# Ten gather buffers instead of six in a four-layer convolution kernel, with shorter projection blocks and two blocks' denominators in one tile

## Chip, cores and metric

The kernel is one program on one core of a Trainium2 chip. The metric is device time in microseconds (us) of one execution, the median of the runs. Engines are called by the profile's names: PE (matrix multiply), DVE (vector), ACT (scalar), POOL (here it only issues gathers), SP (issues all other transfers).

## What is computed

The input is `x`, 4 images of 256 channels on a 64x64 grid, all float32. Four layers follow each other, each of the form `x = x + layer(groupnorm(x))`:

```
layer 0: y  = leaky(bn(conv1x1(x)))
         xp = inproj(y)                       # the table that is sampled
         t  = leaky(bn(depthwise3x3(y)))
         offset, mask = off(t), softmax(mask(t))       # 4 groups x 9 points per pixel
         d  = sum over points of mask * bilinear(xp, base + offset)   # the gather
         x2 = bn(y + outproj(d)); x3 = x2 * se(mean(x2)); y + fc2(leaky(fc1(x3)))
layer 1: q, k, v = relu(bn(conv1x1(x))), and a depthwise 5x5 of each
         out = (v k^T) q / (sum(k) q + eps)   # linear attention, heads of 8 channels
         relu(bn(proj(out)))
layer 2: conv3x3 with binarised weights
layer 3: attention with keys and values max-pooled 2x2, then conv1x1
```

## The kernel before

One image at a time goes through the layers, and work of different images is interleaved. `prepare` makes, for an image, the convolution, the table that is sampled (`tab`, in DRAM: every row holds two vertically adjacent pixels of one group, 512 bytes, and a gather reads two neighbouring rows) and for every sampling point an index and four weights (`s_d`). `sample` gathers and weights. `feedforward` is the rest of layer 0, then come `layer1`, `layer2` and `layer3`.

`run` sets which work lies beside which: `sample(0)` beside `prepare` of images 1 to 3; `sample(1)` beside `first(0)` (feed-forward and layer 1 of image 0); `sample(2)` beside `first(1)` and `second(0)` (layers 2 and 3); `sample(3)` beside `first(2)` and `second(1)`; then `first(3)` beside `second(2)`, and last `second(3)`. `beside` runs the generators in turn: after each step of `sample` (a *unit*), the other works are advanced until their own costs catch up. From this traced order, the dependences and its own estimates a scheduler fixes one instruction order for each engine, and it is not changed at run time. Waits on semaphores are added where they are needed.

`sample` in detail. The pixels of an image are cut into blocks of `BP = RP * BR` pixels (L28 to L30); a *round* is `RP = 14` pixels with 9 points each, so 126 points on the partitions; a unit is `UR = 4` rounds. The 4096 pixels make 293 rounds and 74 units an image. For a block SP loads indices and weights (`sl`, L445, L446) and the residual (`yb`, L448). For a round, POOL issues four indirect transfers (one a group, L465) into one buffer `g` of 4 KB a partition; PE multiplies it with the weights `wm` (made by DVE for a unit, L458), 8 small products a round, 32 a unit, into the PSUM tile `acc` (L472). ACT copies `acc` to `at` (L475), PE transposes it into `dp` (L478), ACT copies that into `dT` (L486). At the end of a block PE multiplies `dT` with the output projection into `po` (L493, two times four products; `po` shares its one PSUM buffer with `dp`), DVE adds it to `yb` (L495), ACT applies the batch norm (L496) and SP stores the block (L498). The tiles `yb` and `dT` have one buffer each, `sl` and `wm` two, `g` six.

`layer1` in detail. A 5x5 depthwise filter (`aggregate`, L600 to L606) is a chain of 25 DVE instructions (L171, L169) into one PSUM tile `agg`, then an ACT copy (L605) into a tile `ak` or `av`, two buffers each. There are 24 of these an image. For the attention output, each chunk of 16 image rows has two blocks `h` of 512 pixels. A block makes a denominator of 64 rows (four products into `den`, L664), adds eps (L666) and takes the reciprocal (L667) on DVE, then for each of four channel groups a product `num` (L671), a product that spreads the reciprocals with the 0/1 matrix `sel` (`rden`, L673), an ACT copy (L674) and a DVE multiplication (L675); the projection follows (L679).

Of the kernel before, what the change touches and what calls it, by code (L numbers as in the profile page):

```python
# [7 lines left out]
F32 = mybir.dt.float32  # L8
I32 = mybir.dt.int32
AF = mybir.ActivationFunctionType  # L10
ALU = mybir.AluOpType
# [4 lines left out]
P = 128  # L16
N, C, H, W = 4, 256, 64, 64
HW = H * W
KT = C // P
NB = HW // 512  # L20
NT = HW // P
G, PT = 4, 9
# [2 lines left out]
NCH = NT // CT  # L25


RP, UR, BR = 14, 4, 36  # L28
RS, BP = RP * PT, RP * BR
BLOCKS = [(p0, min(BP, HW - p0)) for p0 in range(0, HW, BP)]  # L30
OB = 16
# [9 lines left out]
EPS_ATT = 1e-5  # L41
# [24 lines left out]
class Net:  # L66
# [366 lines left out]
    def sample(self, n, ssum):  # L433


        nc, sp = self.nc, self.sp2
        table = self.tab[n].rearrange("g y x s c -> (g y x) (s c)")
        for b, (p0, np_) in enumerate(BLOCKS):
            sl = sp.tile([P, BR, G * 5], F32, name="sl")
            whole, part = np_ // RP, np_ % RP  # L440

            nr = whole + (part > 0)
            rows = self.s_d[n][p0 * PT:p0 * PT + nr * RS, :].rearrange("(r p) f -> p r f", p=RS)
            more = self.s_d[n][p0 * PT + RS:p0 * PT + (nr + 1) * RS, :].rearrange("(r p) f -> p r f", p=RS)
            nc.sync.dma_start(sl[0:RS, 0:nr], rows)  # L445
            nc.sync.dma_start(sl[RS:P, 0:nr], more[0:P - RS])  # L446
            yb = sp.tile([P, KT, BP], F32, name="yb", bufs=1)
            nc.sync.dma_start(yb[:, :, 0:np_], self.y_d[n][:, :, p0:p0 + np_])  # L448
            dT = sp.tile([P, G, BP], F32, name="dT", bufs=1)
            rounds = [(r, RP) for r in range(whole)] + [(whole, part)] * (part > 0)  # L450
            for u in range(0, len(rounds), UR):
                unit = rounds[u:u + UR]
                nu = len(unit)

                wm = self.gp.tile([P, UR, 4 * G, OB], F32, name="wm")
                sh = [P, nu, 4 * G, OB]

                self.tc.keep_in_program_order(nc.vector.tensor_tensor(  # L458
                    wm[:, 0:nu], self.con("own").unsqueeze(1).unsqueeze(1).to_broadcast(sh),
                    sl[:, u:u + nu, G:].unsqueeze(3).to_broadcast(sh), ALU.mult))  # L460
                acc = self.ps1.tile([P, UR, P], F32, name="acc")
                for v, (r, m) in enumerate(unit):
                    g = self.gp.tile([P, G, 256], F32, name="g", bufs=6)
                    for i in range(G):
                        nc.gpsimd.indirect_dma_start(  # L465
                            out=g[:, i, :], out_offset=None, in_=table,
                            in_offset=bass.IndirectOffsetOnAxis(ap=sl.bitcast(I32)[:, r, i:i + 1], axis=0))


                    for x in range(2):  # L470
                        for i in range(G):
                            nc.tensor.matmul(acc[32 * i:32 * i + 32, v, :], wm[:, v, 4 * i + 2 * x:4 * i + 2 * x + 2, :],  # L472
                                             g[:, i, x * P:(x + 1) * P], start=x == 0, stop=x == 1)
                at = sp.tile([P, UR, P], F32, name="at", bufs=1)
                nc.scalar.copy(at[:, 0:nu], acc[:, 0:nu])  # L475
                dp = self.ps1.tile([P, UR, G, 2, OB], F32, name="dp", tag="dp")
                for v in range(nu):
                    nc.tensor.transpose(dp[:, v].rearrange("p g s o -> p (g s o)"), at[:, v], self.ident)  # L478

                full = sum(1 for _, m in unit if m == RP)  # L480
                for v0, v1, m in ((0, full, RP), (full, nu, unit[-1][1])):
                    for s in range(2):
                        if v0 < v1:
                            hs = slice(64 * s, 64 * s + 64)
                            q0 = RP * (u + v0)
                            nc.scalar.copy(  # L486
                                dT[hs, :, q0:q0 + m * (v1 - v0)].rearrange("p g (v o) -> p g v o", o=m),
                                dp[hs, v0:v1, :, s, 0:m].rearrange("p v g o -> p g v o"))
                yield 1
            for m in range(KT):  # L490
                po = self.ps1.tile([P, 512], F32, name="po", tag="dp")
                for k in range(G):
                    nc.tensor.matmul(po[:, 0:np_], self.ow[:, k, m * P:(m + 1) * P], dT[:, k, 0:np_], start=k == 0, stop=k == G - 1)  # L493
                ym = yb[:, m, 0:np_]
                nc.vector.tensor_tensor(ym, po[:, 0:np_], ym, ALU.add)  # L495
                nc.scalar.activation(ym, ym, AF.Identity, bias=self.sh[:, 4 + m:5 + m],  # L496
                                     scale=self.inv[:, 4 + m:5 + m], accum_out=ssum[:, m, b:b + 1])
            nc.sync.dma_start(self.x2_d[n][:, :, p0:p0 + np_], yb[:, :, 0:np_])  # L498
# [51 lines left out]
    def layer1(self, n, st, st2):  # L550
# [3 lines left out]
        with tc.tile_pool(name=f"la{n}", bufs=1, side="right") as sp, \  # L554
# [45 lines left out]
            def aggregate(pd, i, name, func, **more):  # L600

                acc = self.ps1.tile([P, 16, W], F32, name="agg", tag="agg")
                self.depthwise(acc, pd, self.w5[:, i], 5, 16, W, 0, bias=self.b5[:, i:i + 1])
                v = bp.tile([P, 16, W], F32, name=name, tag=name)
                nc.scalar.activation(v, acc, func, **more)  # L605
                return v  # L606

# [41 lines left out]
            for got in rows((0, 1), None, 8):  # L649
                if not isinstance(got, tuple):  # L650
                    yield got
                    continue
                c, qp = got
                aq = []
                for t in range(2):
                    aq.append(aggregate(qp[t], t, ("ak", "av")[t], AF.Relu))
                    yield 28
                for h in range(2):
                    b = 2 * c + h
                    xv = self.block(bp, self.x3_d[n], b, "xr")  # L660
                    qs = [q[:, 2 + 8 * h:10 + 8 * h, 2:W + 2] for q in qp] + [v[:, 8 * h:8 * h + 8, :] for v in aq]
                    pd = self.ps("den")
                    for j in range(4):
                        nc.tensor.matmul(pd[0:64], ld[:, j], qs[j], start=j == 0, stop=j == 3)  # L664
                    rd = bp.tile([64, 512], F32, name="rd", tag="v1")
                    nc.vector.tensor_scalar(rd, pd[0:64], EPS_ATT, None, ALU.add)  # L666
                    nc.vector.reciprocal(rd, rd)  # L667
                    ot = [bp.tile([P, 512], F32, name="ot", tag="kt", bufs=4) for _ in range(4)]
                    for j in range(4):
                        pn = self.ps("num")  # L670
                        nc.tensor.matmul(pn, ln[:, j], qs[j], start=True, stop=True)  # L671
                        pb = self.ps("rden")
                        nc.tensor.matmul(pb, self.con("sel")[0:64, j * P:(j + 1) * P], rd, start=True, stop=True)  # L673
                        nc.scalar.copy(ot[j], pn)  # L674
                        nc.vector.tensor_tensor(ot[j], ot[j], pb, ALU.mult)  # L675
                    for m in range(KT):
                        ps = self.ps()
                        for j in range(4):
                            nc.tensor.matmul(ps, pw[:, j, m * P:(m + 1) * P], ot[j], start=j == 0, stop=j == 3)  # L679
                        r = bp.tile([P, 512], F32, name="pr", tag="v0")  # L680
                        nc.scalar.activation(r, ps, AF.Relu, bias=self.vec("proj_b", m), scale=self.vec("proj_s", m))
                        nc.vector.tensor_tensor(xv[:, m], xv[:, m], r, ALU.add)
                    self.stats(st2, xv, b)
                    nc.sync.dma_start(self.x4_d[n][:, :, b * 512:(b + 1) * 512], xv)
                    yield 20
# [35 lines left out]
    def layer3(self, n, st):  # L721
        nc, tc, a = self.nc, self.tc, self.a
        M = HW // 4
        with tc.tile_pool(name=f"na{n}", bufs=1, side="left") as sp, \
# [32 lines left out]
            for b in range(NB):  # L757
# [3 lines left out]
                    nc.tensor.matmul(ps, tw[:, k], x[:, k], start=k == 0, stop=k == KT - 1)  # L761
                nc.scalar.activation(th[:, b * 512:(b + 1) * 512], ps, AF.Identity, bias=tb)

                m1 = bp.tile([P, KT, 256], F32, name="m1", bufs=1)
                v = x.rearrange("p k (x d) -> p k x d", d=2)
                nc.vector.tensor_tensor(m1, v[:, :, :, 0], v[:, :, :, 1], ALU.max)
                v = m1.rearrange("p k (r d x) -> p k r d x", d=2, x=W // 2)
                xq = bp.tile([P, KT, P], F32, name="xq")
                nc.vector.tensor_tensor(xq.rearrange("p k (r x) -> p k r x", x=W // 2),
                                        v[:, :, :, 0], v[:, :, :, 1], ALU.max)  # L770
                ps = self.ps()
# [101 lines left out]
def arrays(x, **w):  # L873
# [27 lines left out]
    for k in ("theta_b", "phi_b", "wz_b"):  # L901
# [13 lines left out]
        "by": (p[:, None, None] // W + 2 * np.arange(CT)[None, :, None] + d[point % 3][None, None]).reshape(P, -1),  # L915
        "gi": np.broadcast_to((q // PT) * TY * TX + TX + 1, (P, Q)),
        "own": p[:, None] // PT == np.arange(OB)[None],
        "sel": (p[:, None, None] == 16 * np.arange(4)[None, :, None] + p[None, None] // 8).reshape(P, -1),
    }
    rows = np.concatenate([w[l0 + "inproj_b"], w[l0 + "off_b"], w[l0 + "mask_b"], w[l3 + "g_b"]])  # L920
    return {
# [36 lines left out]
```

## Time and profile before

| | us |
|---|---|
| median of 3 runs | 12207.65 (12192.76 to 12220.47) |
| the profiled execution, its own time | 9745.96 |
| its span, first to last instruction | 9744.2 |
| busy in it: PE, DVE, POOL, ACT | 6706.8, 5358.5, 4553.3, 1820.3 |
| mean granted clock of PE, share of full speed | 0.778 |
| gathers in it | 4688, first start 258.0, last start 7349.7 |
| bytes moved | 1052.37 MB, 58% of them by gathers |

The profiled execution is 20% shorter than the median of the runs. A stage below is one image's gathers: S0 from 258 to 1802 us, S1 to 3379, S2 to 5344, S3 to 7351; then the tail to 9744. "Busy" is the union of the instructions' times on an engine. A wait "A <- B" is idle time of A's engine that the end of B ended; its columns are the total in us, the number of times, and the longest in us.

### The profile page before, as it was taken

What the parts mean: (1) busy time and instruction counts of PE and PEld (TensorE: products, weight loads), DVE (VectorE), ACT (ScalarE), POOL (GpSimd) and SP (SyncE); (2) the same over time, 40 slices, a digit from 0 to 9 for tenths busy, and PEclk for the clock granted to TensorE, in tenths of its full rate; (3) what the DMA queues carried; (4) which work ended last, traced back from release to release, by engine and by line L of the source; (5) the groups of instructions that cost most, each with busy time, mean ns of one, the idle gap of its engine ahead of it and who ended that gap; (6) DMA issues with size and microseconds to landing.
All of it is one profiled execution on the core that took longest, in us unless ns stands there. A gap on an engine that the chain in (4) does not pass through costs nothing. (4 is left out here: it accounts for less than half of the span.)

```text
span 9744.2 us, 89537 instructions
## 1 busy us (share of the span) xinstructions
PE 6706.8 (69%) x34636; PEld 3559.7 (37%) x34636; DVE 5358.5 (55%) x6359; ACT 1820.3 (19%) x3546; POOL 4553.3 (47%) x4694
## 2 busy tenths in 40 slices
PE   3567676775557599756676997655778955356797
PEld 2333333343323244333343443333343423233345
DVE  7643444347776624667656226677563287775413
ACT  1111111122211122122221211122121112111112
POOL 0677777777677745656656355656551000000000
PEclk7766677786767799877777897877778977677799
DMA  5665655544335444434333443434332111001110
GB/s 153 174 181 155 169 153 159 149 144 124 114 112 145 119 126 132 113 105 117 108 111 112 127 131 109 118 112 117 100 113 83 61 32 41 15 28 33 42 56 31
DMA packets 795242, 1052.37 MB, mean 108 GB/s; under 512 B 462144, under 2 KB 502208, under 8 KB 793024
## 3 DMA queue, kind: packets, MB, share of 16 engines
q0 software_dynamic: 225024, 614.77, 21.9%
q1 hardware_dynamic: 569792, 431.88, 15.3%
q8 instruction: 273, 4.47, 0.2%
q14 instruction: 153, 1.25, 0.0%
HBM read 878.36 MB, written 167.90 MB: 107 GB/s over the span
## 5 line engine op out<-in xcount | busy, mean ns | idle before, releaser
L465 POOL DMA_INDIRECT g<-tab,sl x4688 | 4552.6, 971 | 2796.7 <-issue 1324.2
L169 DVE SCALAR_TENSOR_TENSOR agg<-pad,vec,agg 128x1024 f32<-128x1024 f32 x2560 | 3294.2, 1287 | 65.5 <-ACT pad L356 1.2
L472 PE MATMUL acc<-g,wm 128*32 128x128 f32 x18752 | 1351.0, 324 | 856.1 <-DMA g<-tab,sl 715.6
L472 PEld LDWEIGHTS acc<-g,wm 128*32 128x32 f32 x18752 | 744.2, 124 | 1569.1 <-DMA g<-tab,sl 1139.2
L711 PE MATMUL ps<-xp,w 128*128 128x512 f32 x2304 | 1025.0, 598 | 20.8 <-ACT xp L705 20.8
L711 PEld LDWEIGHTS ps<-xp,w 128*128 128x128 f32 x2304 | 432.2, 191 | 534.4 <-issue 513.0
L617 PE MATMUL pt<-ident,av 128*128 128x128 f32 x256 | 88.9, 405 | 767.1 <-ACT av L605 767.1
L475 ACT COPY at<-acc 128x512 f32<-128x512 f32 (+1 forms) x296 | 172.1, 581 | 2224.4 <-PE acc L472 2224.0
L536 PE MATMUL ps<-x2f,f 128*128 128x512 f32 x1024 | 466.9, 607 | 5.1 <-ACT f L528 5.1
L458 DVE TENSOR_TENSOR wm<-con,sl 128x1024 f32<-128x1024 f32 (+1 forms) x296 | 354.4, 1207 | 199.8 <-PE acc L472 199.7
L543 PE MATMUL ps<-hm,f 128*128 128x512 f32 x1024 | 453.4, 594 | 0.0
L160 DVE SCALAR_TENSOR_TENSOR hm<-ps,vec,lk 128x512 f32<-128x512 f32 x256 | 192.2, 751 | 441.6 <-ACT lk L159 438.4
L801 PE MATMUL pt<-ident,pe 128*128 128x128 f32 x1024 | 201.8, 342 | 331.1 <-ACT pe L794 330.2
L806 PE MATMUL ps<-gt,pT 128*128 128x128 f32 x2048 | 392.5, 368 | 32.7 <-DVE pT L803 26.4
L582 PE MATMUL ps<-xr,qw 128*128 128x512 f32 x768 | 390.7, 638 | 6.4 <-DMA xr<-x 6.4
L159 ACT ACTIVATE lk<-ps,low 128x512 f32<-128x512 f32 x320 | 219.7, 687 | 929.4 <-PE ps L536 615.2
L806 PEld LDWEIGHTS ps<-gt,pT 128*128 128x128 f32 x2048 | 363.4, 274 | 76.0 <-DVE pT L803 68.8
L171 DVE TENSOR_SCALAR agg<-pad,vec,b 128x1024 f32<-128x1024 f32 x96 | 129.0, 1344 | 414.6 <-ACT pad L352 272.3
L617 PEld LDWEIGHTS pt<-ident,av 128*128 128x128 f32 x256 | 53.7, 214 | 778.6 <-ACT av L605 778.6
L715 DVE TENSOR_TENSOR x<-x,ps 128x512 f32<-128x512 f32 x64 | 43.9, 686 | 480.9 <-PE ps L711 480.9
L478 PE MATMUL dp<-ident,at 128*128 128x128 f32 x1172 | 234.9, 334 | 100.2 <-ACT at L475 99.6
L801 PEld LDWEIGHTS pt<-ident,pe 128*128 128x128 f32 x1024 | 142.0, 171 | 435.3 <-ACT pe L794 432.6
(225 smaller groups left out, 7418.5 us busy)
## 6 DMA issues: line engine op xcount, KB each, us to landing
x<-x SPq DMA_DIRECT2D x160, 512.0 KB
g<-tab,sl POOLq DMA_INDIRECT x4688
xr<-x SPq DMA_DIRECT2D x128, 512.0 KB
x<-in_x SPq DMA_DIRECT2D x64, 512.0 KB
tab<-xo SPq DMA_DIRECT2D x512, 64.0 KB
y<-yc SPq DMA_DIRECT2D x32, 512.0 KB
x2f<-x SPq DMA_DIRECT2D x32, 512.0 KB
xyf<-x SPq DMA_DIRECT2D x32, 512.0 KB
```

The source lines that it names most:

```text
L159: nc.scalar.activation(t, ps, AF.Identity, bias=low, scale=SLOPE)
L169: nc.vector.scalar_tensor_tensor(acc, s, wt, acc, ALU.mult, ALU.add)
L458: self.tc.keep_in_program_order(nc.vector.tensor_tensor(wm[:, 0:nu], self.con("own").unsqueeze(1).unsqueeze(1).to_broadcast(sh), sl[:, u:u ...
L465: nc.gpsimd.indirect_dma_start(out=g[:, i, :], out_offset=None, in_=table, in_offset=bass.IndirectOffsetOnAxis(ap=sl.bitcast(I32)[:, r, i: ...
L472: nc.tensor.matmul(acc[32 * i:32 * i + 32, v, :], wm[:, v, 4 * i + 2 * x:4 * i + 2 * x + 2, :], g[:, i, x * P:(x + 1) * P], start=x == 0, ...
L478: nc.tensor.transpose(dp[:, v].rearrange("p g s o -> p (g s o)"), at[:, v], self.ident)
L536: nc.tensor.matmul(ps, f1[:, k, m * P:(m + 1) * P], x2[:, k], start=k == 0, stop=k == KT - 1)
L543: nc.tensor.matmul(ps, f2[:, k, m * P:(m + 1) * P], hm[:, k], start=k == 0, stop=k == 4 * KT - 1)
L582: nc.tensor.matmul(ps, qw[:, k, t * P:(t + 1) * P], x[:, k], start=k == 0, stop=k == KT - 1)
L711: nc.tensor.matmul(ps, w[:, k, t, m * P:(m + 1) * P], xp[:, k, t // 3:t // 3 + 8, t % 3:t % 3 + W], start=i == 0, stop=i == KT * 9 - 1)
L801: nc.tensor.transpose(pt[:, m], pe[:, (4 * i + m) * P:(4 * i + m + 1) * P], self.ident)
L806: nc.tensor.matmul(ps[:, 0:P], pT[:, m], gt[:, m], start=m == 0, stop=m == 7)
```

## The change

`BR` goes from 36 to 20, so a block has 280 pixels and not 504, and an image 15 blocks and not 9. `g` gets ten buffers. To make further room, `ak` and `av` share three buffers under one tag instead of two each, and in layer 3 `m1` and `xq` use the buffers of `pe` and `m2`. In layer 1 the denominators of the two blocks of a chunk are made first, one in partitions 0 to 63 and one in 64 to 127 of one tile; one addition and one reciprocal serve both, and `sel` is repeated in the upper half so that each block takes its own.

```diff
-RP, UR, BR = 14, 4, 36
+RP, UR, BR = 14, 4, 20
...
-                    g = self.gp.tile([P, G, 256], F32, name="g", bufs=6)
+                    g = self.gp.tile([P, G, 256], F32, name="g", bufs=10)
...
-                v = bp.tile([P, 16, W], F32, name=name, tag=name)
+                v = bp.tile([P, 16, W], F32, name=name, tag="ag", bufs=3)
...
+                qh = [[q[:, 2 + 8 * h:10 + 8 * h, 2:W + 2] for q in qp] + [v[:, 8 * h:8 * h + 8, :] for v in aq] for h in range(2)]
+                pd = self.ps("den")
+                for h in range(2):
+                    for j in range(4):
+                        nc.tensor.matmul(pd[64 * h:64 * h + 64], ld[:, j], qh[h][j], start=j == 0, stop=j == 3)
+                rd = bp.tile([P, 512], F32, name="rd", tag="v1")
+                nc.vector.tensor_scalar(rd, pd, EPS_ATT, None, ALU.add)
+                nc.vector.reciprocal(rd, rd)
                 for h in range(2):
                     b = 2 * c + h
+                    hs = slice(64 * h, 64 * h + 64)
                     xv = self.block(bp, self.x3_d[n], b, "xr")
-                    qs = [q[:, 2 + 8 * h:10 + 8 * h, 2:W + 2] for q in qp] + [v[:, 8 * h:8 * h + 8, :] for v in aq]
-                    pd = self.ps("den")
-                    for j in range(4):
-                        nc.tensor.matmul(pd[0:64], ld[:, j], qs[j], start=j == 0, stop=j == 3)
-                    rd = bp.tile([64, 512], F32, name="rd", tag="v1")
-                    nc.vector.tensor_scalar(rd, pd[0:64], EPS_ATT, None, ALU.add)
-                    nc.vector.reciprocal(rd, rd)
+                    qs = qh[h]
...
-                        nc.tensor.matmul(pb, self.con("sel")[0:64, j * P:(j + 1) * P], rd, start=True, stop=True)
+                        nc.tensor.matmul(pb, self.con("sel")[hs, j * P:(j + 1) * P], rd[hs], start=True, stop=True)
...
-                m1 = bp.tile([P, KT, 256], F32, name="m1", bufs=1)
+                m1 = bp.tile([P, KT, 256], F32, name="m1", tag="pe")
...
-                xq = bp.tile([P, KT, P], F32, name="xq")
+                xq = bp.tile([P, KT, P], F32, name="xq", tag="m2")
...
-        "sel": (p[:, None, None] == 16 * np.arange(4)[None, :, None] + p[None, None] // 8).reshape(P, -1),
+        "sel": (p[:, None, None] % 64 == 16 * np.arange(4)[None, :, None] + p[None, None] // 8).reshape(P, -1),
```

## The prediction

> **What bounds the kernel now.** I read the busy slices of the page first, then busy times by stage, then the waits of POOL and of PE in each stage, and last the groups by form.
>
> ```profile
> PE   3567676775557599756676997655778955356797
> ...
> POOL 0677777777677745656656355656551000000000
> ```
>
> POOL is level at 7 for slices 1 to 13 (S0, S1), then falls to 3 to 6 (S2, S3). Two regimes, then, which the table by stage separates (PE, PEld, DVE, ACT, POOL busy, with instruction counts):
>
> ```profile
> core 0: us, PE busy (x) PEld busy (x) DVE busy (x) ACT busy (x) POOL busy (x), PEclk, DMA share, GB/s
> 0.00:258.00 258.00, 100.71 (x340) 63.99 (x340) 188.65 (x257) 33.69 (x59) 0.69 (x6) 0.76 0.58 152
> 258.00:1802.00 1544.00, 1020.14 (x6116) 516.61 (x6117) 679.56 (x936) 214.03 (x434) 1163.88 (x1172) 0.68 0.58 163
> 1802.00:3379.00 1577.00, 995.79 (x6591) 512.22 (x6590) 1021.04 (x976) 311.00 (x600) 1136.16 (x1172) 0.75 0.45 130
> 3379.00:5344.00 1965.00, 1443.45 (x8298) 787.31 (x8296) 1120.00 (x1279) 411.54 (x812) 1126.99 (x1173) 0.80 0.40 116
> 5344.00:7351.00 2007.00, 1476.90 (x8319) 796.84 (x8317) 1135.28 (x1309) 419.06 (x827) 1125.60 (x1172) 0.81 0.40 116
> 7351.00:9744.00 2393.00, 1669.79 (x4977) 882.74 (x4977) 1213.93 (x1605) 430.97 (x815) 0.00 (x0) 0.82 0.13 41
> ```
>
> A gather takes a median 0.946 us and another follows 0.304 us later ("issue"), so one each 1.25 us; 1172 are 1465 us at least, 20 us a unit. S0 and S1 stand just above that: **POOL paces them**. S2 and S3 take 26.5 us a unit: there the chain of PE, DVE and ACT paces. POOL's waits in S1 and in S2:
>
> ```profile
> POOL g L465 <- issue: 334.5, 1098, 0.3
> POOL g L465 <- PE acc L472: 92.2, 28, 18.1
> ```
> ```profile
> POOL g L465 <- PE acc L472: 494.4, 44, 46.1
> POOL g L465 <- issue: 325.3, 1068, 0.3
> ```
>
> Waiting for `acc` means that all six buffers are full and PE is late (S0: 27.9 us, S3: 536.3). The 494 is no gain to be had: POOL waits because PE is slower. What counts in S2 is where PE itself stands still:
>
> ```profile
> PE pt L617 <- ACT av L605: 173.9, 8, 33.3
> PE acc L472 <- DMA g<-tab,sl: 91.4, 120, 2.1
> ```
>
> PE stands 33 us at a time before transposes that need a filter chain of DVE (25 x 1.287 us). Six buffers are 24 gathers, 30 us: POOL fills them and stops, and later, when several units follow closely, PE runs the buffers dry and waits for gathers, 91.4 us in S2 and 91.9 in S3. Only that part can deeper buffering return. In the tail there is no gather; DVE's filters and PE's products alternate, and PE waits there for the reciprocal:
>
> ```profile
> PE rden L673 <- DVE rd L667: 36.2, 10, 4.2
> ```
>
> [...]
>
> **The change part by part**, against the profiled execution's own 9745.96 us.
>
> *Ten buffers.* 40 gathers, 50 us of lead. The order of instructions keeps 1172 gathers an image on POOL and 293 x 8 products on PE; on PE whole units of 32 stand together more often (in image 0, 54 of them against 29). S1: of the stops of 92.2 us none is over 18.1, under the 20 us of added lead, and PE is quick enough behind them (996 of 1577 busy): minus 80, bounds 40 and 92. S0: 27.9, of which 23.4 in one stop after the first gathers: minus 25, bounds 0 and 28. S2 and S3: at most PE's waits for gathers, 91.4 + 91.9 = 183; at least 0, where the next thing that PE needs is late anyway. In PE's instruction order S2 has some five places where two to four units stand almost side by side (4 to 16 other products between them), most after stretches of 50 to 90 others; one more unit ready at each would save up to 20 us, so all 91 are within reach if nothing else is late. I take two thirds of 183: minus 120. What is late next is `av`.
>
> *Shorter blocks.* 24 more block ends (60 for 36). PE: 504-wide products and 64-wide ones of L493 cost 255.0/512 = 0.498 and 12.3/64 = 0.192 us of union time. The line through both gives 0.342 for 280 columns and 0.270 for 176: 896 x 0.342 + 64 x 0.270 = 324 for 267, plus 57. PE's idle time before these products, 26.6 us in 36 ends, is 0.74 an end: plus 18. DVE's additions: 0.678 and 0.219 give 0.443 at 280 columns, 7 us more in all; ACT's norms likewise 27 (0.807 and 0.187 for 504 wide). SP: 96 more transfers at 0.5 us of issue, 48 us spread over 7100; its stores wait on `yb` (326 us), now for shorter pieces, and behind them stand loads for the other works; nobody is shown waiting for those but `xp` in the tail, where no block is stored. I take 0, bounds minus 20 and plus 40. In S0 and S1 PE's added time hides behind POOL's pace; in S2 and S3 half of 75 shows: plus 37. If that cover is gone, all 75 count.
>
> *Denominators.*
>
> ```profile
> L667 DVE RECIPROCAL rd<-rd 64x512 f32<-64x512 f32 x32 | 107.0, 3345 | 1.1
> ...
> L666 DVE TENSOR_SCALAR rd<-den 64x512 f32<-64x512 f32 x32 | 21.8, 683 | 118.4 <-PE den L664 118.4
> ```
>
> 16 of each go: 16 x 4.03 = 64 us of DVE. A 128-row form of L667 isn't in the trace; other DVE rows cost the same for 64 and 128 rows (0.683 and 0.692 at 512 columns), so 3.35, and at worst 6.7, which takes the gain away. Products are as many as before, four of them now ahead of the first reciprocal (4 x 0.6 = 2.4 us later) and not between the blocks. On the path I count half of PE's waits for `rd`: 18 in the tail, 18 of 37 in S2 and S3. Minus 36, bounds 0 and 64.
>
> *Three buffers for `ak` and `av`.* The third tile after an `ak` is the next chunk's `av`; ACT's copy then waits for the last `num` on `ak`, and DVE's next chain for that copy, since `agg` has one buffer. In the tail the first copy comes at 8612.0, its last `num` at 8665.5, the next `av` at 8767.6: 100 us to spare. 0. *`m1`, `xq`:* they live in the first loop of layer 3, `pe` and `m2` in the second; 0. *wm, sl:* same counts; blocks turn over each 100 us while `sl` has two buffers; 0.
>
> Sum: -80 - 25 - 120 + 37 - 36 = minus 224 us, 2.3% of the profiled execution. The median is 2462 us above it and I don't know which engine takes that time. If all scaled, 281 would be saved; I take the saving as it stands: 12207.65 - 224 = **11984**.
>
> **Rivals.**
> *PE is the bound in the runs (slower).* If the 2462 us are PE's, its waits for gathers vanish: in S1 to S3 PE is busy 3916 us and waits 142.1 + 91.4 + 91.9 = 325 for gathers; what is left to gain falls below the block ends' cost less the denominators' (75 - 36 = 39) once PE is 286 us, or 7%, slower there. Then the 24 block ends stand open: 75 x 1.25 = 94, less 18 for the tail's denominators: about 12283. For it: a gap of 25% is more than 7. Against: nothing in the trace shows PE slower, and PE's clock of 0.80 leaves S0 and S1 to POOL.
> *Gathers are the bound in the runs (no change).* If the gap is all theirs, a gather takes (12207.65 - 258 - 2393) / 4688 = 2.04 us; six buffers are then 49 us, over nearly all of PE's delays, and only the tail's 18 us go: 12190. For it: POOL paces two stages as it is. Against: then all four stages would have to be paced so.
> *Everything scales and all waits go.* 28 + 92 + 183 + 64, at no cost of block ends, times 1.25: minus 459, 11749.
> *The change doesn't do what it says:* the built program has the ten buffers' gathers in the same order on POOL, so only an unseen wait on `sl` could cap the lead; it would give the second rival's time.
>
> **How the numbers follow.** The forecast 0.53, full scaling 0.09, gathers 0.14 (as often a little faster), PE-bound 0.24. Faster by over 0.2% (24 us, about what a measurement of this kernel tells from no change): 0.62; within: 0.14; slower: 0.24. The range from 11770 to 12310 takes in the forecast with its bounds, both rivals above it, and most of full scaling. The forecast's own range is 11880 to 12120.
>
> **What would show it.** Right: POOL's waits for `acc` near zero in S1 and S0, stages of 1520 and 1500 us; PE's waits for gathers in S2 and S3 under 70 together; L667 16 times at about 3.35 us; L493 960 times at near 0.34. Wrong: S2 and S3 as long as before with PE's waits moved to `av`; POOL waiting for `sl`; ACT's L605 waiting for `num`; or a median that rises while the profiled execution falls.

## The result: no difference, and the profile after

The changed kernel takes 12234.51 us (median of 4, 12218.36 to 12264.03), the kernel before 12214.06 beside it: a ratio of 1.0022 with a 95% interval of 0.9999 to 1.0046. A second measurement with 22 runs against 27 (e9) gives 12217.89 against 12206.01, 1.0007 (0.9996 to 1.0018). Nothing is gained; 224 us were forecast.

One fact is needed to read all that follows: the pace of this kernel goes with the chip. On chips 1 and 11 the kernel before takes 12.2 ms in every one of its runs (12164 to 12245 us), on chips 3 and 12 it takes 9.73 ms in every one (9713 to 9748). No chip showed both; only chip 12 was used at two times, and it kept its pace. The profile on which the forecast was built is an execution of the second sort, while the median to be forecast, and with it the first runs and the first profile of the changed kernel, are of the first. Below they are called the **short pace** (9.7 ms) and the **long pace** (12.2 ms).

The busy slices of the changed kernel's page, to be held against those of before:

```profile
PE   3444444573444567655445667655346678545697
...
POOL 1555656444564543443444333443444310000000
```

POOL no longer stands at a level 7 in the first third; by the table it is busy 58% of S0 (1134.71 of 1948) and 41% of S3. The table by stage (columns as in that of before):

```profile
core 0: us, PE busy (x) PEld busy (x) DVE busy (x) ACT busy (x) POOL busy (x), PEclk, DMA share, GB/s
0.00:262.00 262.00, 106.49 (x340) 66.94 (x340) 189.66 (x259) 33.78 (x59) 0.82 (x7) 0.72 0.55 148
262.00:2210.00 1948.00, 834.51 (x6085) 515.61 (x6086) 676.12 (x942) 216.70 (x453) 1134.71 (x1172) 0.64 0.47 129
2210.00:4404.00 2194.00, 1111.23 (x6716) 599.27 (x6715) 996.93 (x973) 315.51 (x622) 1118.45 (x1172) 0.68 0.33 94
4404.00:7117.00 2713.00, 1584.79 (x8351) 872.33 (x8351) 1095.71 (x1276) 420.00 (x838) 1113.67 (x1173) 0.73 0.29 84
7117.00:9848.00 2731.00, 1592.27 (x8393) 876.93 (x8391) 1118.07 (x1308) 423.12 (x848) 1114.97 (x1172) 0.73 0.30 85
9848.00:12228.00 2380.00, 1652.62 (x5137) 884.87 (x5137) 1222.59 (x1619) 434.08 (x822) 0.12 (x1) 0.82 0.13 41
```

The tail lasts 2380 us, against 2393 in the short execution of before. The whole difference of 2.4 ms lies in the four stages with gathers, and hardly an engine is busier there (PE 5123 us for 4936 in the four): nearly all of it is idle time. The waits of the whole span (total in us, times, longest):

```profile
ACT at L475 <- remote: 3587.1, 259, 64.4
POOL g L465 <- PE acc L472: 3361.0, 205, 67.3
POOL g L465 <- issue: 1303.2, 4268, 2.0
PE dp L478 <- issue: 1219.0, 200, 26.2
...
PE acc L472 <- DMA g<-tab,sl: 28.3, 28, 2.3
```

Three things are to be read here. POOL waits 3361 us for `acc`; in that time all ten buffers are full. PE waits 28.3 us in all for gathers, and that is the wait that deeper buffering can remove; in the profile of before it was 715.6. This figure alone would not do, since the trace holds the records of only part of the landings (see "What stays open"), and PE's further 632.7 us before these products go to "issue", nothing shown. The records of the transfers themselves are complete (225024 packets of gathers, 48 for each, taken in order) and settle it: the first product of a round starts a median 60 us after the last packet of its gathers has landed (27 us in e1, with six buffers; 7 us in the profile of before, and 2 us before that landing or earlier in a quarter of its rounds). And ACT's copy `at` is released late: it starts a median 6.2 us after the last recorded product of its unit, in the profile of before 0.09 us. "Remote" means here that the semaphore's update comes too long after every instruction that makes it for the view to name one; it is the one that the products of `acc` update, in every such case of this profile and of e1. What PE's transposes `dp` wait for is not shown. The groups that the change touches:

```profile
L493 PE MATMUL po<-dT,ow 128*128 128x280 f32 x896 | 336.6, 534 | 154.5 <-DVE yb L495 84.1 <-ACT dT L486 42.4 <-issue 21.0
...
L666 DVE RECIPROCAL rd<-rd 128x512 f32<-128x512 f32 x16 | 53.6, 3353 | 0.5
```

### The profile page after: what moved, and what is told of

Its sections match the earlier page's. It is cut to its first block, busy times and chain, and to the rows that moved or that the text cites. A ratio compares the mean times of both kernels' runs of the same rounds, so it can differ in the third digit from the quotient of the medians.

```text
span 12228.0 us, 90771 instructions
## 1 busy us (share of the span) xinstructions
PE 6881.9 (56%) x35020; PEld 3815.9 (31%) x35020; DVE 5299.1 (43%) x6375; ACT 1843.2 (15%) x3642; POOL 4482.7 (37%) x4694
## 3 DMA queue, kind: packets, MB, share of 16 engines
q0 software_dynamic: 225024, 614.77, 17.6%
## 5 line engine op out<-in xcount | busy, mean ns | idle before, releaser
L465 POOL DMA_INDIRECT g<-tab,sl x4688 | 4482.1, 956 | 5364.8 <-PE acc L472 3361.0
L169 DVE SCALAR_TENSOR_TENSOR agg<-pad,vec,agg 128x1024 f32<-128x1024 f32 x2560 | 3295.1, 1287 | 85.6 <-ACT pad L356 21.4
L472 PE MATMUL acc<-g,wm 128*32 128x128 f32 x18752 | 1057.4, 327 | 789.9 <-issue 632.7
L478 PE MATMUL dp<-ident,at 128*128 128x128 f32 x1172 | 312.7, 418 | 2007.8 <-issue 1219.0
L472 PEld LDWEIGHTS acc<-g,wm 128*32 128x32 f32 x18752 | 702.9, 130 | 1209.6 <-issue 954.8
L715 PE MATMUL ps<-xp,w 128*128 128x512 f32 x2304 | 1055.8, 611 | 19.9 <-DMA xp<-x 12.1
L478 PEld LDWEIGHTS dp<-ident,at 128*128 128x128 f32 x1172 | 200.6, 208 | 2185.3 <-issue 1348.4
L475 ACT COPY at<-acc 128x512 f32<-128x512 f32 (+1 forms) x296 | 171.9, 581 | 3923.2 <-remote 3587.1
L536 PE MATMUL ps<-x2f,f 128*128 128x512 f32 x1024 | 544.6, 683 | 99.9 <-DVE hm L160 55.7
L582 PE MATMUL ps<-xr,qw 128*128 128x512 f32 x768 | 434.1, 702 | 17.5 <-DVE gt L781 10.7
L493 PE MATMUL po<-dT,ow 128*128 128x280 f32 (+1 forms) x960 | 352.6, 525 | 158.4 <-DVE yb L495 85.0
L536 PEld LDWEIGHTS ps<-x2f,f 128*128 128x128 f32 x1024 | 215.8, 220 | 387.6 <-issue 271.0
```

The source lines that it names most:

```text
L169: nc.vector.scalar_tensor_tensor(acc, s, wt, acc, ALU.mult, ALU.add)
L465: nc.gpsimd.indirect_dma_start(out=g[:, i, :], out_offset=None, in_=table, in_offset=bass.IndirectOffsetOnAxis(ap=sl.bitcast(I32)[:, r, i: ...
L536: nc.tensor.matmul(ps, f1[:, k, m * P:(m + 1) * P], x2[:, k], start=k == 0, stop=k == KT - 1)
L582: nc.tensor.matmul(ps, qw[:, k, t * P:(t + 1) * P], x[:, k], start=k == 0, stop=k == KT - 1)
L715: nc.tensor.matmul(ps, w[:, k, t, m * P:(m + 1) * P], xp[:, k, t // 3:t // 3 + 8, t % 3:t % 3 + W], start=i == 0, stop=i == KT * 9 - 1)
```

## Experiments

### The parts, each by itself, in the long pace

**e1**, the kernel before unchanged, for a profile of the long pace.

> The kernel before, unchanged, for a profile of it at the pace of the timed runs (about 12210 us); the one shown so far lasted 9746. Theory A (late hand-over): as in the profile after, ACT's copy of acc (L475) starts a median 6 us after the last product of a unit is recorded, where the short execution shows 0.1; 296 units at 6 to 8 us are 1800 to 2400 us, the gap. POOL then waits for acc about 3000 us and PE for gathers little. Theory B (slow gathers): a gather takes up to 2.0 us on POOL or lands late, POOL does not wait for acc, and L475 follows its products at once. Theory C (slow PE): L711 and L536 take over 15% longer per product all through the program, the tail included.

12182.11 us. Stages of 1866, 2133, 2738 and 2771 us, a tail of 2412. In the record of this run ACT's copy of a unit starts a median 5.9, 5.7, 6.2 and 6.2 us (S0 to S3) after the unit's last product; in the short execution it is 0.09 us. PE waits 14.7 us for gathers in all, as far as landings are recorded.

```profile
POOL g L465 <- PE acc L472: 3331.9, 205, 73.6
ACT at L475 <- remote: 3183.3, 256, 32.9
...
PE acc L472 <- DMA g<-tab,sl: 14.7, 12, 2.5
```

With six buffers POOL stops 205 times for `acc`, with ten also 205 times. Both traces have 312 stretches of gathers without a stop of over 1.5 us, the median 16 long, which is one unit. At each stop the buffers are full either way, and PE gives about one unit free.

**e2**, the new denominators alone: one tile for the two blocks of a chunk, `sel` repeated.

```diff
...
-                    rd = bp.tile([64, 512], F32, name="rd", tag="v1")
...
+                rd = bp.tile([P, 512], F32, name="rd", tag="v1")
...
```

> Only the shared denominators; 504-pixel blocks, six gather buffers, own buffers for ak, av, m1 and xq. Forecast's term: minus 36 us (0 to 64), ratio 0.997. Theory A: DVE and PE have slack beside the late hand-overs in the stages with gathers, so only the tail's 18 us show, ratio 0.9985. Rival: a 128-row reciprocal costs double or the longer den group delays, ratio 1.000 or above.

12090.23 us against 12191.65, a ratio of 0.9907 (0.9889 to 0.9926), the best of all in the long pace and faster than both kernels. By the profiles of e1 and e2, 45 us come from the tail (2367 for 2412) and 38 from S3. It was forecast at 36 us in all.

**e3**, the shorter blocks alone: `RP, UR, BR = 14, 4, 20`.

> Only BR = 20: 60 block ends for 36, six gather buffers, old denominators. Forecast's term: plus 37 to 75 us, ratio 1.003 to 1.006. If block ends also suffer late hand-overs (dp, po): 24 more ends at 5 us and more, plus 120 us, ratio 1.010. If nothing: 1.000.

12261.33 us, 1.0050 (1.0031 to 1.0068): a loss of 38 to 83 us.

**e4**, e3 with the ten buffers and what makes room for them (three buffers for `ak` and `av`, the tags of `m1` and `xq`), the old denominators.

```diff
...
-                    g = self.gp.tile([P, G, 256], F32, name="g", bufs=6)
+                    g = self.gp.tile([P, G, 256], F32, name="g", bufs=10)
...
```

> Ten gather buffers with BR = 20, three buffers for ak and av, and the shared ones for m1 and xq; old denominators. Against the short blocks alone this shows the buffers. Forecast: minus 225 us against the short blocks, ratio about 0.985 to the kernel before. Theory A: POOL waits for acc in every stage whatever the number of buffers, PE is never short of gathers, so no gain: same as short blocks alone within 0.2%.

12348.08 us, 1.0128 (1.0103 to 1.0153), 87 us more than e3. The two profiled executions lie 42 us apart, 33 of them in the tail (2431 us for 2398): POOL is further ahead when it ends, so after the last gather 144 products are recorded in place of 80. Whether the loss is the buffers' or the room's was not separated in the long pace. The parts multiply to 0.9907 x 1.0128 = 1.0034, close to the 1.0007 to 1.0022 of the whole: the change is a gain of about 0.9% and losses of about 1.3% that cancel.

### What the long pace is

The first idea was that the late copy is the cause: 296 units x 6 us = 1780 us of the 2462. Two readings of it were to be told apart, products that run one after the other (A), and a late hand-over (B).

**e5**, half of the products left out, those with `x = 1`; the output lacks their share.

```diff
-                    for x in range(2):
+                    for x in range(1):
...
```

> The kernel before with half of the acc products left out (x=0 only, 16 a unit for 32; the output then lacks the x=1 corners). Theory A, one after the other: in the usual pace the four column parts do not overlap and each acc product takes PE about 0.24 us (from the first recorded start to ACT's copy of a unit are 1.68 + 6.21 us, over 32 products), though the recorded starts stand 0.053 us apart. Then the copy starts about 3 us after the last product for 6.2, PE is freed of 9376 x 0.24 = 2250 us, and the time falls to 9.9 to 10.5 ms, with S0 and S1 back at the gathers' pace of 1.25 us each (about 1500 us). Theory B, a fixed lateness of the hand-over, whatever the products: the delay stays at 6 us and the time falls by the recorded 500 us at most, to 11.7 ms or more.

**e6**, products over the full width, as many as before, each of them into all of `acc` (so the sums are not those of the kernel).

```diff
-                            nc.tensor.matmul(acc[32 * i:32 * i + 32, v, :], wm[:, v, 4 * i + 2 * x:4 * i + 2 * x + 2, :],
-                                             g[:, i, x * P:(x + 1) * P], start=x == 0, stop=x == 1)
+                            nc.tensor.matmul(acc[:, v, :], wm[:, v, 8 * x:8 * x + 8, :],
+                                             g[:, i, x * P:(x + 1) * P], start=x + i == 0, stop=x + i == G)
```

> The kernel before with the same number of acc products and the same columns moved, each with 128 weight columns over all of acc, in place of 32 columns into a quarter of it (the sums are other ones than the reference's). [...]Theory A: they already run one after the other, so the time stays at 12.1 to 12.4 ms. Theory B: they overlap four at a time at 0.053 us, and only the hand-over is late; then 18752 products become some 0.16 us longer, 3000 us of PE, and the time is 13.7 to 15.2 ms.

Both ran on chip 12, where the kernel before takes 9735.63 us, so A and B could not be told apart as planned. What they gave is another thing. e5: 9767.51 us (one run), no gain from 9376 recorded products fewer (the trace holds two records of each product, 18752 in all). e6: 9809.02 us (one run). There the products of a unit start 0.22 us apart and a unit takes a median 7.4 us from its first product to the copy in S2, where the short execution of before takes 2.7. Five microseconds more at the very place where the long pace loses six cost 73 us here, not 1780 (PE's granted clock was 0.86 for 0.78 here, and its 512-column products took 595 ns for 598 at L711, 599 for 607 at L536 and 603 for 638 at L582; what that gives back was not measured). So the late copy by itself doesn't explain the long pace, and the first idea fell. e11 below says the same from the long pace.

**e7**, the operands exchanged: `g` as weights, 32 columns of `wm` moving; no copy `at` and no transposes.

```diff
...
+                            nc.tensor.matmul(acc[:, v, i].rearrange("p s o -> p (s o)"), g[:, i, x * P:(x + 1) * P],
+                                             wm[:, v, 4 * i + 2 * x:4 * i + 2 * x + 2, :].rearrange("p s o -> p (s o)"),
+                                             start=x == 0, stop=x == 1)
...
```

> The kernel before with the two operands of the acc products exchanged: g's 128 channels are the weights and wm's 32 columns move, so that acc comes out as dp would; the 1172 transposes, the copy at and its hand-over go, and nothing is left out of the computation. 32 columns move for 128 in each product, but 18752 weight loads are of 128 columns for 32. [...]Theory B: the late hand-over stays, one a unit, now before the copies to dT; 296 times a copy and a transpose wait of some 2.5 us go: about 11.4 ms, with a delay still near 6 us.

10856.38 us in the short pace, 1.1151 (1.1134 to 1.1168): with 18752 recorded weight loads of 128 columns in place of 32, PE is busy for 8757 us, where it was 6707: 3385 for 1351 in these products, and a load takes 281 ns for 124. It says nothing of the long pace and is no better kernel.

**e9**, the changed kernel again, gave the second measurement above. **e10** and **e11** ran beside it on chip 1, in the long pace.

> The changed kernel once more. The pace belongs to the chip: e5 to e8 ran where the kernel before takes 9736 us, e1 to e4 where it takes 12192, with copies at that start 6 us after the last product. If the kernel before takes about 9740 here, the forecast's sum is tried on its own ground: 9740 - 224 = 9516 if the ten buffers save what was forecast; about 9680, as with six buffers (e8), if they save nothing. If the kernel before takes about 12190 here, POOL waits for PE either way and the time is 12200 to 12260.

**e10**, half of the gathers left out: `for i in range(2)` around the transfer, `g[:, i % 2, ...]` in the product, so two of the four groups are sums of the wrong rows.

> The kernel before with two of the four gathers of a round left out; the products of the other two groups read the two tiles that are there (so their sums are other ones). What is looked at is the delay from a unit's last recorded acc product to ACT's copy. Theory G: in the long pace PE's hand-overs wait behind POOL's gathers (the copies start as a gather's issue ends, a median of five gathers later): with half as many gathers the delay falls to 3 us or less and the time to 9.5 to 10.5 ms. Theory P: the delay comes from the dense products alone: it stays at 6 us, and the time falls by no more than the 200 to 400 us of waits for gathers. In the short pace the delay is 0.1 us already, and S0 and S1 fall to PE's pace, some 1100 us each, about 9.0 ms.

10424.01 us (one run). Each theory got one half right. The delay stayed at a median 5.3 to 6.2 us, as P said; but 1782 us went, not 200 to 400, as G said (how much of it would go in the short pace too was not measured). The delay goes with gathers: in 251 of the 271 units with a delay of 3 to 20 us the copy starts after five or six gathers of a stretch; in e1 it is five to seven in 172 of 243. It starts about as a gather's issue ends (in e1 a median 0.94 us after the gather's start, and a gather takes 0.96). In e10 most stretches are only six or eight gathers long, so there the copy may as well wait for the end of the stretch.

**e11**, the products read a constant, so that POOL doesn't wait for PE.

```diff
-                                             g[:, i, x * P:(x + 1) * P], start=x == 0, stop=x == 1)
+                                             self.ident, start=x == 0, stop=x == 1)
```

> The kernel before with all its gathers and all its acc products, but the products read the identity matrix in place of g, so that neither PE waits for gathers nor POOL for PE (the sums are other ones). Theory G: POOL issues one gather each 1.25 us without a stop, and in the long pace the copies at are late as before wherever gathers run; S0 and S1 last 1470 us, but gathers that run ahead end early and later units are on time. Theory P: the delay of 6 us stays in all four stages, also after the gathers have ended, 12 ms in all. In the short pace: about 9.4 to 9.6 ms.

14307.37 us (one run). All waits between PE and the gathers are gone, and the kernel is 17% **slower**. POOL now issues a whole block, 144 gathers, in one stretch of 180 us. The busy table of two such stretches, each with what follows it:

```profile
core 0: us, PE busy (x) PEld busy (x) DVE busy (x) ACT busy (x) POOL busy (x), PEclk, DMA share, GB/s
...
3075.80:3256.00 180.20, 41.57 (x121) 16.75 (x119) 7.64 (x10) 4.57 (x9) 136.60 (x144) 0.58 0.39 113
3256.00:3449.30 193.30, 113.77 (x746) 65.46 (x746) 96.00 (x115) 41.29 (x76) 0.04 (x1) 0.77 0.12 34
3449.30:3629.40 180.10, 34.26 (x151) 17.09 (x150) 27.01 (x23) 10.51 (x23) 136.51 (x144) 0.58 0.40 113
3629.40:3786.80 157.40, 55.21 (x637) 40.18 (x638) 114.32 (x101) 28.72 (x58) 0.07 (x2) 0.63 0.06 14
```

The counts in brackets tell it: PE starts 121 products while POOL issues and 746 in the pause after it, DVE 10 and 115, ACT 9 and 76. PE's products and weight loads (PEld) in the timeline of the first stretch (start, duration, what, and in brackets the idle time before it):

```profile
3113.67 1.92 PE L472 MATMUL acc<-ident,wm 128*32 128x128 f32 x26 [13.88 <-issue]
...
3144.15 0.37 PE L472 MATMUL acc<-ident,wm 128*32 128x128 f32 x1 [2.43 <-issue]
...
3145.55 0.13 PEld L472 LDWEIGHTS acc<-ident,wm 128*32 128x32 f32 x1 [2.67 <-issue]
...
3146.95 0.37 PE L472 MATMUL acc<-ident,wm 128*32 128x128 f32 x1 [2.43 <-issue]
...
3148.35 0.13 PEld L472 LDWEIGHTS acc<-ident,wm 128*32 128x32 f32 x1 [2.67 <-issue]
...
3149.75 0.37 PE L472 MATMUL acc<-ident,wm 128*32 128x128 f32 x1 [2.43 <-issue]
```

26 products are through in 1.92 us, and then one comes each 2.80 us, for 100 us, its weight load half way, so that one of the two passes each 1.40 us. The trace shows nothing that these products wait for, and they read no gathered tile. The copies `at` follow the last recorded product of their unit by a median 0.12 us here, and the kernel is slower all the same. So it is not only a hand-over that is late: **while POOL issues gathers without a stop, the instructions of the other engines pass at a crawl**, on this chip. It holds over all of e11 (a stop of over 1 us ends a stretch): in 100 us of such stretches PE starts 70 recorded products, and 438 in 100 us between them (DVE 11 and 66 instructions, ACT 6 and 40); in the profile of before it is 406 and 453 (64 and 61, 38 and 34).

Theory G pointed to the right place, with too small an effect. What in a run of gathers holds the others up is not separated: POOL's issuing, the transfers and the records of their landings come together in every run. The amount of traffic alone is not it. Before the first gather the transfers move 148 GB/s in the changed kernel's profile and 152 in that of before, and this stretch lasts 262 and 258 us.

e11 itself was not run in the short pace, but no such thing is seen there with POOL equally busy; the changed kernel on chip 3 (e15, same columns), in two pieces of 180 us:

```profile
1900.00:2080.00 180.00, 180.00 (x983) 90.22 (x974) 57.91 (x77) 42.88 (x78) 137.33 (x141) 1.00 0.52 155
2300.00:2480.00 180.00, 75.18 (x805) 54.59 (x806) 140.59 (x129) 37.98 (x77) 133.55 (x138) 0.69 0.40 114
```

### The change on the ground of the forecast: the short pace

**e8**, **e12** and **e16**, the changed kernel with six buffers (`bufs=6`, all else as changed), on chips 12, 3 and 12. e12 and e16 were meant for the long pace.

> The changed kernel with six gather buffers, all else as changed. If PE paces the gathers (theory A or B alike), ten buffers bring nothing: within 25 us of the changed kernel, 12210 to 12260 us, and the extra 87 us of buffers and room together are the room's. If the ten buffers themselves cost, by what the earlier gathers collide with: 12130 to 12160.

> The changed kernel with six gather buffers once more (e8 had it on a chip of the short pace, 57 us under the kernel before). Theory G says that in the long pace hand-overs between engines stand still while POOL issues gathers without a stop (e11: 144 gathers, 180 us, with at most two copies at). Ten buffers only lengthen those stretches, so against the changed kernel (ratio 1.0007) six give a gain: 0.993 to 0.999 of the kernel before. If buffers don't count at all: 1.000 to 1.002. In the short pace: 0.994 again.

> The changed kernel with six gather buffers, to have it beside a kernel before of 12.2 ms (e8 and e12 were of 9.74: 0.994). The changed kernel itself is 1.0007 there. Theory G, the stretches of gathers stop the other engines: six buffers give 0.993 to 0.999. If buffers don't count in the long pace: 1.000 to 1.002.

9678.27, 9680.54 and 9674.73 us: 0.9941, 0.9942 and 0.9942 of the kernel before (0.9927 to 0.9956 over all three). What these runs were to tell of the long pace stays open; in the short pace the new denominators, the shorter blocks and the room save 54 us together.

**e15**, the changed kernel, beside e12 on chip 3.

> The changed kernel as it is. Where the kernel before takes about 9740 us: 9516 if the forecast's sum holds on the ground on which it was made, about 9680 if ten buffers save nothing there. Where it takes about 12200: 0.999 to 1.004 of it, as in e9.

9390.31 us, 0.9640 (0.9625 to 0.9654): **344 us less** than the kernel before, 290 less than with six buffers. The waits of POOL in S0, of POOL in S1, and of PE in S2 and in S3:

```profile
POOL g L465 <- DMA sl<-sd: 40.2, 2, 20.2
POOL g L465 <- DMA g<-tab,sl: 9.8, 32, 0.3
POOL g L465 <- PE acc L472: 5.9, 9, 3.4
```
```profile
POOL g L465 <- issue: 331.7, 1088, 0.3
POOL g L465 <- PE acc L472: 31.0, 26, 12.6
```
```profile
PE pt L617 <- ACT av L605: 174.1, 8, 33.3
PE pt L805 <- ACT pe L798: 76.8, 29, 6.2
PE acc L472 <- DMA g<-tab,sl: 37.9, 53, 2.1
```
```profile
PE acc L472 <- DMA g<-tab,sl: 39.7, 57, 1.9
```

POOL's 92.2 us in S1 have become 31.0, PE's 91.4 and 91.9 us have become 37.9 and 39.7, and what is late next is `av`, as the forecast said. In S0 the stops for `acc` are down to 5.9 us, but POOL now waits 40.2 us, in two stops, for a block's indices (`sl`), which it does in neither profile with six buffers (before and e12). The stages last 1557, 1522, 1844 and 1857 us.

**e13** and **e17**, the new denominators with four buffers (chips 3 and 12); meant for the long pace as well.

> The kernel before with the new denominators alone (e2: 0.9907 in the long pace) and four gather buffers in place of six: 16 gathers are the longest stretch after POOL has stopped. Theory G: shorter stretches, hand-overs less late, below e2: 0.96 to 0.985. If POOL's lead is what counts (the change's own reasoning): above e2, 1.00 to 1.03, as PE waits for gathers more often. In the short pace, where hand-overs are in time, only the second holds: 1.00 to 1.03.

> New denominators and four gather buffers, beside a kernel before of 12.2 ms (e13 was beside 9.73: 1.024, as PE waits more for gathers). Theory G: stretches of 16 gathers in place of 24, hand-overs less late, 0.96 to 0.985. If the lead counts in the long pace as well: 1.00 to 1.03; if neither, as e2: 0.991.

9970.19 and 9966.46 us, 1.0238 (1.0224 to 1.0252) and 1.0244 (1.0230 to 1.0258). PE waits 999.6 us for gathers where the kernel before, with six buffers, has 715.6 and the changed kernel, with ten, 531.5; POOL waits 1423.0 us for `acc` where they have 1150.7 and 775.8. These kernels differ in blocks or denominators too, but in the short pace the lead is worth time on both sides.

**e14** and **e18**, a memset of 128 x 64 on POOL after each gather (chips 3 and 12), also meant for the long pace.

```diff
+        nap = self.gp.tile([P, 64], F32, name="nap", bufs=1)
...
+                        nc.gpsimd.memset(nap, 0.0)
```

> The kernel before with a small memset (128 x 64) on POOL after each gather, 4688 of them, of some 0.1 to 0.2 us each. If work of POOL between the gathers lets the hand-overs of the long pace through, the delay of the copies at falls from 6 us to 1 or 2 and the time to 10 to 11 ms. If only a stop of POOL does (a wait), the delay stays, each gather's slot is longer by the memset, and the time grows by up to 4688 x 0.2 = 900 us. In the short pace S0 and S1 grow by 1172 x 0.1 to 0.2 each, 250 to 500 us in all.

> A memset on POOL after each gather, beside a kernel before of 12.2 ms (e14 was beside 9.73: 672 us more). If work of POOL between gathers lets the hand-overs through, the delay of the copies at falls from 6 us to 1 or 2 and the time to 10.5 to 11.3 ms. If only a stop of POOL does, the delay stays and the time is 12.2 to 13.1 ms.

10406.68 and 10398.05 us, 1.0687 and 1.0689. The memsets take 155 ns each, 724.6 us in all, and the time grew by 672, more than the 250 to 500 expected; S1 alone grew by 441, which 1172 memsets of 155 ns (182 us) don't explain; that stays open. Whether such work lets the other engines through in the long pace was not seen.

## Why the prediction was wrong

**The step that failed** is the one that carries the sum over to the runs: "The median is 2462 us above it and I don't know which engine takes that time. If all scaled, 281 would be saved; I take the saving as it stands". The sum was about a balance (POOL paces S0 and S1; PE runs dry in S2 and S3) that doesn't exist in the runs which were to be forecast: there POOL stops 3.3 ms for full buffers, and the gathers of a round have long landed when PE comes to them. The gap of 2462 us was larger than all the waits in the sum, and it was all in the stages that the change touches. It was treated as a remark when it was the main fact. One of the forecast's own signs of being wrong, "a median that rises while the profiled execution falls", describes what came: 344 us less in the short pace, and 12 more, within the noise, in the long one.

Point by point, the forecast against the two paces:

| step | forecast | short pace (e12, e15) | long pace (e1 to e4, e9) |
|---|---|---|---|
| ten buffers | -225 | -290 | with the room +87 |
| shorter blocks | +37 (75 at most) | not alone | +70 (38 to 83) |
| denominators | -36 (0 to 64) | not alone | -101 (-135 to -90 by the ratio) |
| blocks, room and denominators | +1 | -54 | |
| sum | -224 | -344 | +12 (-5 to +22 by the ratio) |

*Ten buffers.* Right in mechanism for S1 to S3 on its own ground, and somewhat small: by the profiles of e12 and e15 these are 120, 100 and 98 us shorter, and PE's waits for gathers in them fell by 109, 86 and 76. S0 was forecast 25 us shorter and is 25 longer: the stops for `acc` fell by 22 (28.3 to 5.9), but the 40.2 us for `sl` came. The term of `sl` was put at nothing because "blocks turn over each 100 us while `sl` has two buffers"; with the longer lead that failed. The tail is 27 us longer and was not in the sum; why is not shown, as 80 recorded products are left after the last gather with six and with ten buffers. By the waits, the whole term is empty in the long pace. PE waits 14.7 us for gathers in e1's records, where the forecast found 325 in S1 to S3, and POOL stops 205 times for full buffers with six and with ten alike.

*Shorter blocks.* "If that cover is gone, all 75 count": in the long pace POOL paces no stage, which fits, and 70 were measured. That the two lie so near is partly luck. From e1 to e3 PE's time in L493 grew by 64 us and its idle time before it by 107, where 57 and 18 were counted. The 280-column products take 336.6 us for 896 in the changed kernel's profile, 0.376 each, and 0.286 in e15, where 0.342 was worked out. Nor did POOL's pace hide the block ends in the short pace: with six buffers S1 is 65 us longer in e12 (1642) than before (1577), and POOL's stops in it are 160.9 us for 92.2. This includes the room and the denominators, which no run takes apart there.

*Denominators.* Mis-sized. The reciprocal of 128 rows takes 3353 ns, the 3.35 us that was taken. The term counted half of PE's waits for `rd` and so 18 us in the tail; the tail lost 45 (e2 against e1). That blocks no longer wait one after the other for a denominator was said and not priced. PE's wait for `rd` in the tail fell by 15 us, from 36.2 to 20.9; the other 30 are not itemised.

*The rivals.* "PE is the bound in the runs" had the right signature, PE's waits for gathers gone and the block ends open, and it gave 12283 with a chance of 0.24. Its cause is not what was found: PE's long products are nearly as quick (512 columns in layer 2: 611 ns for 598; in the feed-forward beside gathers, L536, 683 for 607), it is the passing of instructions beside POOL's gathers that is slow (one product each 2.80 us in e11). "Against: nothing in the trace shows PE slower" was true of the trace and no argument, as that trace was not of the runs. "Gathers are the bound in the runs" gave 12190 and no change: nearest by number, but POOL waits 3361 us for `acc`, so gathers bound nothing.

*The clock.* The ratio 1.253 of the median to the profiled execution (12207.65 / 9745.96) does not come from slower engines all through: the filter step L169 (DVE) takes 1287 ns and the copy L475 (ACT) 585 or 586 ns in both paces, and the tail is about as long in both (2393 us in the profile of before, 2412 in e1). PE's granted clock is lower in the long pace (0.72 over the span for 0.78), but that is not the gap either: PE's busy time grew by 376 us from the profile of before to e1 (7083 for 6707), of 2436, and e7 had 0.717 on a chip of the short pace.

*What stays open.* Why some chips are of the long pace. While gathers run, the traces of the long pace also lack most records of landings: 15594 from gathers in the changed kernel's, 74135 in e15's. Before the first gather and in the tail none are missing (3394 and 3136 from other transfers, 3393 and 3136 in e15). All runs here, the timed ones too, come with a recorded span and clock, so none shows the kernel without recording. That the recording itself holds the engines up on these chips is therefore a rival that no run excludes; records go missing just where the instructions crawl, and in e11 one recorded instruction of PE passes each 1.40 us. Nor was it seen whether fewer buffers or pauses help there.

## What to carry to other kernels

Before working out a sum from a profile, hold its own time against the runs: if it is 20% off, the profile is of another regime, and the sum has to be made for each regime with the chance of each, or not at all. A gap that size need not be spread evenly; here each stage with gathers had its share and the tail none, which one profile of the long pace shows at once. And count a buffer's worth by the consumer's wait for it (15 or 716 us here for the same program, the kernel before), not by the producer's stops for full buffers: where ten buffers saved 120, 100 and 98 us in a stage, PE's waits had fallen by 109, 86 and 76.

## What was unexpected of the hardware

- Two paces of one program on chips of one kind: 9713 to 9748 us on two of them, 12164 to 12245 on two others, with single instructions equally long (L169 1287 ns, L475 586 ns, a gather 0.97 or 0.96 us).
- On a chip of the long pace the other engines slow down while POOL issues gathers without a stop: in e11 PE goes to one product each 2.80 us, with 70 started in 100 us of such stretches and 438 between them, and 17% more time for a program with fewer dependences. The gathers themselves are as quick, a median 2.4 us from issue to the last packet in both paces.
- A reciprocal of 128 rows costs what one of 64 rows costs: 3353 and 3345 ns at 512 columns.
